# Two of seven half-block products, each made by seven quarter-block products

## The chip, the cores and the metric

The kernel runs on one core of one Trainium2 chip. The metric is the device time of one execution in microseconds. TensorE (PE in the profile) multiplies, with its weight loads shown as PEld; VectorE is DVE, ScalarE ACT, GpSimd POOL, SyncE SP. Everything is float32.

## The reference

Four graph layers run one after the other on x of 128 graphs x 64 nodes x 256 features (8192 tokens in all), each on relu(layernorm(x)) and each added to x. The change touches two places.

Layer 0 ends in LSTMs over windows of length p = 1, 2, 3, 4, with weights of their own for each length, the later ones reading what the earlier have written:

```python
def step(carry, x_t):
    h, c = carry
    g = x_t @ Wih.T + h @ Whh.T + bias          # 256 -> 4 x 256
    i, f, gg, o = jnp.split(g, 4, axis=-1)
    c = jax.nn.sigmoid(f) * c + jax.nn.sigmoid(i) * jnp.tanh(gg)
    h = jax.nn.sigmoid(o) * jnp.tanh(c)
...
for p in range(1, MAX_SKIP + 1):
    wins = h[:, :nw * p, :].reshape(Bv * nw, p, Hd)
    last = _lstm_last(Wih[p-1], Whh[p-1], bih[p-1], bhh[p-1], wins)
    h = h.at[:, jnp.arange(nw) * p + (p - 1), :].set(last.reshape(Bv, nw, Hd))
```

Layer 3 is three times "multiply by a weight, then mix the nodes with adj * adj", with widths 256 -> 512 -> 1024 -> 256 and a relu after the first two:

```python
h = relu(slconv(x, adj, adj, W1)); h = relu(slconv(h, adj, adj, W2)); return slconv(h, adj, adj, W3)
```

Layers 1 (attention) and 2 (a graph convolution with batch norms) lie between them and keep their code.

## The kernel before, in words

**Seven products in place of eight.** A weight block of 2x2 halves, (a11 a12; a21 a22), times an input of 2x2 halves, (b11 b12; b21 b22), needs seven half-block products instead of eight, if sums of the weight halves (`sums`, L228) and differences of the input halves (`differences`, L216) are made first (the Winograd form of Strassen's method). Products 1 to 7 are (a11,b11), (a12,b21), (s4,b22), (a22,t4), (s1,t1), (s2,t2), (s3,t3). `seven` makes them in four PSUM banks: products 1, 5, 6 and 7 first; ACT copies 1 and 5 to SBUF (p1, p5; L181, L182), DVE adds 6 to p1 and 7 to p5 (L184, L185); then `finish` lets POOL add p1 and p5 into the output block 1,1 (L189), adds product 2 into the bank of product 1 for block 0,0, product 3 into that of 5 and product 4 into that of 7, and DVE adds p1 to the last two (L195, L199). `end` is the activation that closes a block.

**LSTM.** Two units (256 windows x 2 blocks each, 224 at length three) are worked in pairs, pair j of each length p. `first_steps` makes step 0, which has no hidden state; `next_step` makes steps t >= 1 of one unit: four input differences (L709 to L714), then two calls of `gate_set`, one for the gates i and g and one for f and o, then cell and hidden state (L721 to L724, `output`). In a gate set of `next_step` the halves of the contraction are x and h, each of two chunks of 128, so one product is four matmuls of 128x128 weights with 128x256 inputs. `blocks_of` makes the weight sums once a length. Lengths one to four have 8, 8, 6 and 4 units.

**Layer 3.** 16 groups of 512 tokens. In each, `second_weights` (512 -> 1024, matmuls at L1599) makes two sets (q = 0 and 2) of seven products, again four matmuls of 128x128 with 128x256 each; the first four products of both sets come before the last three of either. `third_weights` (L1649) follows, with matmuls of 128x128 inputs.

**Order.** The tile framework orders each engine's instructions when the kernel is built: by program order among those that are ready by its own estimate of durations, so that an engine may take a later instruction first. On the chip each engine then keeps that order. There are eight PSUM banks, which is two sets. `tc.issue_after(x)` keeps what follows behind x on its engine. x tiles of the first four groups (tags x0 to x3) are loaded at the start and stay in SBUF until the layer's output is added to them, by DMAs of POOL (L293) in the last pair of length four.

Of the kernel before, what the change touches and what calls it, by code (L numbers as in the profile page):

```python
# [15 lines left out]
P = 128  # L16
# [23 lines left out]
def adj_preln_kernel(ctx: ExitStack, tc: tile.TileContext, x_in, adj, vec, bg0, bg1,  # L40
# [128 lines left out]
    def summed_last():  # L169
        return sums_on_pool[-1]  # L170

    def seven(products, banks, p1, p5, out, end, parts=lambda b: [b]):
# [9 lines left out]
        copied = nc.scalar.copy(p5, ps[1])  # L182

        nc.vector.tensor_tensor(p1, p1, ps[2], ALU.add)  # L184
        added = nc.vector.tensor_tensor(p5, p5, ps[3], ALU.add)  # L185

        def finish():
            sums_on_pool.append(
                nc.gpsimd.tensor_tensor(out=out[1][1], in0=p1, in1=p5, op=ALU.add).ins  # L189
            )  # L190
            end(1, 1, None)
            products[2](ps[0], False)
            end(0, 0, ps[0])
            products[3](ps[1], False)
            nc.vector.tensor_tensor(out[0][1], p1, ps[1], ALU.add)  # L195
            end(0, 1, None)
            products[4](ps[3], False)
            for to, p, q in zip(*(parts(b) for b in (out[1][0], p1, ps[3]))):
                last = nc.vector.tensor_tensor(to, p, q, ALU.add)  # L199
# [116 lines left out]
    with tc.tile_pool(name="lw", bufs=5) as lw:  # L316
# [242 lines left out]
        with tc.tile_pool(name="back", bufs=1, reuse_waits="tile") as back_pool, \  # L559
# [22 lines left out]
            def gate_set(p, n, g, gates, w, bs):  # L582

                pairs = [sevens(w, b, lambda *wb: wb) for b in bs]

                def product(i):
                    def issue(ps, first):
                        for r, j, _ in gates:  # L590
                            for c, (wc, bc) in enumerate(zip(*pairs[r][i])):
                                nc.tensor.matmul(  # L592
                                    ps[:, r], lhsT=wc[:, j, :], rhs=bc,
                                    start=first and r == 0 and c == 0, stop=True,
                                    skip_group_check=True,
                                )

                    return issue

                out = [[g[:, :, m, blk, 0:n] for blk in range(2)] for m in range(2)]  # L600
                p15 = lp.tile([P, 2, 2, 256], F32, tag="p15", name="p15")
                same = gates[0][1:] == gates[1][1:]

                def act(o, ps, j, m, func):
                    col = (p - 1) * 8 + 2 * j + m
                    nc.scalar.activation(o, ps, func, bias=lbias[:, col : col + 1])  # L606
# [10 lines left out]
                return seven(  # L617
                    {i: product(i) for i in range(1, 8)}, [bank((P, 2, 256))[:, :, 0:n] for _ in range(4)],
                    p15[:, 0, :, 0:n], p15[:, 1, :, 0:n], out, end,
                )  # L620

            def output(t, p, u, gate_o, th):
# [78 lines left out]
            def next_step(t, p, n, u, ws, last_sum=None):  # L701

                x_of, cell, hid = u
                tt = dp.tile([P, 4, 2, 256], F32, tag="diff", name="diff")
# [9 lines left out]
                nc.vector.tensor_tensor(ts[3], h1, ts[1], ALU.subtract)  # L714
                if last_sum is not None:
                    last_sum()
                b = (by_chunk([x1]) + [None], by_chunk([h1, h2]), by_chunk(ts))
                ig, fo = gate_tile(), gate_tile()
                gate_i, gate_g, gate_f, gate_o = (g[:, r, :, :, 0:n] for g in (ig, fo) for r in range(2))
                gate_set(p, n, ig, [(0, 0, AF.Sigmoid), (1, 2, AF.Tanh)], ws, [b] * 2)()  # L720
                nc.vector.tensor_tensor(gate_i, gate_i, gate_g, ALU.mult)  # L721
                gate_set(p, n, fo, [(0, 1, AF.Sigmoid), (1, 3, AF.Sigmoid)], ws, [b] * 2)()
# [13 lines left out]
            def blocks_of(p, wi, wh):  # L736
# [14 lines left out]
                return ws, lambda: make([3])  # L751


            stepped = None
            w0 = first_blocks(
                w_next[0], lw.tile([P, 2, 1024], F32, tag="w", name="s"), copied_of[5:9]
            )
            for p, nk in ((1, 8), (2, 8), (3, 7), (4, 8)):
                n = nk * HB
                wi, wh = w_next  # L760
# [5 lines left out]
                for j in range(0, len(units), 2):  # L766
                    two = [unit(p, *u, nk) for u in units[j : j + 2]]
                    first_steps(p, n, two, units[j : j + 2], w0)
                    if p > 1:
                        flush()  # L770
                        if j == 0:
                            ws, last_sum = blocks_of(p, wi, wh)
                    if j + 2 == len(units):
                        if p < 4:
                            w0 = first_blocks(
# [3 lines left out]
                        else:  # L779
# [7 lines left out]
                            nc.vector.tensor_tensor(ss[0], wqk[1][0], wqk[1][1], ALU.add)  # L787
                            nc.vector.tensor_tensor(ss[1], ss[0], wqk[0][0], ALU.subtract)
                            nc.vector.tensor_tensor(wdiff, wqk[0][0], wqk[1][0], ALU.subtract)
                    for t in range(1, p):  # L790
                        for i, u in enumerate(two):
                            stepped_before = stepped
                            stepped = next_step(
                                t, p, n, u, ws, last_sum if (j, t, i) == (0, 1, 0) else None
                            )

                            if p == 4 and j == 2:
# [781 lines left out]
            order=[(2, (2, 3, 0, 1)), (0, range(GT))],  # L1579
        )  # L1580

    def second_weights(m1, room):

        h2 = [arena(ar_right) for _ in range(2)]
# [4 lines left out]
        tt = arena(ar_right).rearrange("p i (c n) -> p i c n", c=2)  # L1589
        ts = [tt[:, i] for i in range(4)]  # L1590
        last = differences(nc.vector, *act[0], *act[1], *ts)

        def products(q):
            def product(w, b):
# [15 lines left out]
        for q in (0, 2):  # L1610
            p1, p5 = (room[:, q + i, :].rearrange("p (r n) -> p r n", r=2) for i in range(2))
            blocks = [
                [h2[m][:, q : q + 2, n * HN : (n + 1) * HN] for n in range(2)] for m in range(2)
            ]
            ends.append(
                seven(
                    products(q), [bank((P, 2, HN)) for _ in range(4)], p1, p5, blocks,
                    ends_in(blocks, AF.Relu),
                )
            )  # L1620
        for end in ends:
# [5 lines left out]
    def third_weights(h2, parts=lambda b: [b]):  # L1627
# [1 line left out]

        last = arena(ar_right)  # L1630
        s3 = last[:, 0:2, :].rearrange("p a (b d) -> p (a b) d", d=D)
        act = [[h2[c][:, :, m * HN : (m + 1) * HN] for c in range(2)] for m in range(2)]
        s_tiles = [arena(ar_right) for _ in range(2)]
        ss = [
            s_tiles[i // 2][:, 2 * (i % 2) : 2 * (i % 2) + 2, :].rearrange(
# [78 lines left out]
                ready += 1  # L1714

    AHEAD = 4
    a, finish_start = first_start()
    s3, scaled = None, None
    for g in range(NG + 1):
# [106 lines left out]
```

## Time and profile before

| | |
|---|---|
| median of three runs | 2432.34 us (2431.85 to 2433.87) |
| the profiled execution | 2432.54 us |
| its span, first to last instruction | 2430.8 us |
| PE, PEld busy | 2409.7 us, 2088.7 us |
| DVE, ACT, POOL busy | 1546.7, 1130.2, 497.5 us |
| L592, matmuls of the LSTM | 156.9 to about 1200 us of the span |
| L1599, matmuls of `second_weights` | 16 groups from 1680.6 us on, about 24.3 us each |
| granted TensorE clock | 0.999 |

A line of the timeline has start, duration (both us), engine, line of the code, operation, tiles out<-in, shape and count of instructions merged into it, and in brackets the idle time of the engine just before it, with what ended it. A group of merged matmuls is shown up to the end of its last one's pipeline, so the next one's start, not start plus duration, tells how fast they follow each other. A matmul of 128*128 weights with 128x256 inputs in float32 shows as two records. `x2` on other engines means two instructions.

### The profile page before, as it was taken

How to read it: one execution, taken by the hardware profiler on the slowest of the kernel's cores; microseconds unless marked ns; L12 is line 12 of the kernel's file. 1: busy time of each engine (PE TensorE's matmuls, PEld its weight loads, DVE VectorE, ACT ScalarE, POOL GpSimd, SP SyncE). 2: the span in 40 equal slices, each digit the busy share in tenths (PEclk: the TensorE clock that was granted, in tenths of full speed). 3: DMA queues.
4: the chain of work that ended last, by engine and by line, in shares of the span. 5: the costliest groups of instructions: out<-in, count | busy, mean ns of one | idle time of the engine just before them, and what ended most of it. 6: DMA issues, size and time to landing. Idle time of an engine off the chain costs nothing.

```text
span 2430.8 us, 46867 instructions
## 1 busy us (share of the span) xinstructions
PE 2409.7 (99%) x19648; PEld 2088.7 (86%) x19648; DVE 1546.7 (64%) x2829; ACT 1130.2 (46%) x2022; POOL 497.5 (20%) x445
## 2 busy tenths in 40 slices
PE   9999999999999999999999999999999999999999
PEld 6778888889999998888888867586988898999898
DVE  6768866666566575575599888576655445444543
ACT  4557755444445343353455565564343333333332
POOL 4432211111111111112224445123111111111100
PEclk9999999999999999999999999999999999999999
DMA  4200000001000000143246410010233100000000
GB/s 140 84 2 1 1 18 1 1 1 35 1 1 1 1 1 1 18 96 70 48 82 129 78 29 2 10 61 10 36 53 62 27 10 19 10 10 11 18 10 19
DMA packets 161587, 73.21 MB, mean 30 GB/s; under 512 B 104416, under 2 KB 157792, under 8 KB 161376
## 3 DMA queue, kind: packets, MB, share of 16 engines
q1 hardware_dynamic: 147984, 57.08, 9.5%
q0 software_dynamic: 12672, 12.58, 3.5%
q8 instruction: 154, 2.52, 0.4%
q10 hardware_dynamic: 720, 0.56, 0.1%
q14 instruction: 57, 0.47, 0.1%
HBM read 40.84 MB, written 20.97 MB: 25 GB/s over the span
## 4 chain that ended last, share of the span: by engine, by line
PE 92%; DVE 5%; ACT 2%; issue 1%; DMA 0%; POOL 0%; ACTq 0%; DVEq 0%; POOLq 0%
PE ps L592 41%; PE ps L1599 16%; PE ps L1649 8%; PE ps L1556 4%; PE ps L146 4%; PE ps L952 3%; PE ps L501 2%; PE ps L527 2%; PE ps L1326 2%; PE ps L878 2%; PE ps L911 2%; PE ps L1388 1%; PE ps L974 1%; PE ps L1670 1%; PE ps L1354 1%
## 5 line engine op out<-in xcount | busy, mean ns | idle before, releaser
L592 PE MATMUL ps<-diff,s 128*128 128x256 f32 (+1 forms) x1824 | 393.5, 371 | 0.9 <-DVE diff L713 0.9
L1599 PE MATMUL ps<-arena 128*128 128x256 f32 x1792 | 391.4, 380 | 0.0
L1599 PEld LDWEIGHTS ps<-arena 128*128 128x128 f32 x1792 | 338.9, 190 | 48.2 <-issue 2.0
L592 PEld LDWEIGHTS ps<-diff,s 128*128 128x128 f32 x1824 | 345.9, 190 | 33.8 <-issue 1.6
L606 ACT ACTIVATE gates<-gates,lbias 128x512 f32<-128x512 f32 (+5 forms) x426 | 244.1, 620 | 200.5 <-DVE gates L195 144.8
L189 POOL TENSOR_TENSOR gates<-p 128x512 f32<-128x512 f32 (+1 forms) x115 | 148.6, 1292 | 882.0 <-DVE p L185 831.1
L592 PE MATMUL ps<-h,w 128*128 128x256 f32 (+1 forms) x1028 | 241.0, 371 | 0.0
L592 PE MATMUL ps<-diff,w 128*128 128x256 f32 (+1 forms) x1040 | 238.7, 370 | 0.0
L189 POOL TENSOR_TENSOR arena<-arena 128x512 f32<-128x512 f32 (+1 forms) x80 | 91.1, 1139 | 613.7 <-DVE arena L185 601.4
L592 PEld LDWEIGHTS ps<-diff,w 128*128 128x128 f32 x1040 | 197.4, 190 | 18.2
L592 PEld LDWEIGHTS ps<-h,w 128*128 128x128 f32 x1028 | 195.0, 190 | 19.2 <-issue 0.5
L606 ACT ACTIVATE gates<-ps,lbias 128x256 f32<-128x256 f32 (+3 forms) x213 | 91.8, 477 | 247.2 <-PE ps L592 247.0
L239 ACT ACTIVATE arena<-arena 128x512 f32<-128x512 f32 x144 | 88.5, 628 | 250.4 <-POOL arena L189 163.1
L195 DVE TENSOR_TENSOR gates<-p,ps 128x512 f32<-128x512 f32 (+1 forms) x115 | 76.3, 664 | 114.3 <-PE ps L592 114.0
L1649 PE MATMUL ps<-arena 128*128 128x128 f32 x1280 | 148.4, 275 | 0.0
L1649 PEld LDWEIGHTS ps<-arena 128*128 128x128 f32 x1280 | 146.5, 192 | 0.9
L184 DVE TENSOR_TENSOR arena<-arena,ps 128x512 f32<-128x512 f32 (+1 forms) x80 | 48.2, 602 | 138.5 <-PE ps L1599 50.0
L195 DVE TENSOR_TENSOR arena<-arena,ps 128x512 f32<-128x512 f32 (+1 forms) x80 | 48.1, 602 | 125.5 <-PE ps L1599 57.6
L228 DVE TENSOR_TENSOR arena<-arena 128x512 f32<-128x512 f32 (+1 forms) x192 | 108.2, 597 | 21.9 <-ACT arena L239 20.2
L592 PE MATMUL ps<-state,w 128*128 128x256 f32 (+1 forms) x512 | 116.1, 370 | 0.9 <-ACT p L181 0.8
L184 DVE TENSOR_TENSOR p<-p,ps 128x512 f32<-128x512 f32 (+1 forms) x131 | 86.9, 663 | 47.4 <-PE ps L592 46.6
L199 DVE TENSOR_TENSOR gates<-p,ps 128x512 f32<-128x512 f32 (+1 forms) x115 | 76.6, 666 | 62.9 <-PE ps L592 62.4
(219 smaller groups left out, 4127.1 us busy)
## 6 DMA issues: line engine op xcount, KB each, us to landing
x<-in_x SPq DMA_DIRECT2D x19, 512.0 KB, 4.1
y<-turned SPq DMA_DIRECT2D x64, 128.0 KB, 3.7
v<-vt SPq DMA_DIRECT2D x128, 64.0 KB, 2.3
w<-in_wih SPq DMA_DIRECT2D x4, 1024.0 KB, 8.4
x_for_h<-in_x SPq DMA_DIRECT2D x8, 512.0 KB, 6.6
x<-y POOLq DMA_DIRECT2D x8, 512.0 KB, 6.3
x_for_h<-y POOLq DMA_DIRECT2D x8, 512.0 KB, 6.8
z<-w SPq DMA_DIRECT2D x64, 64.0 KB, 2.0
```

The lines of the kernel that those rows point to most:

```text
L146: last = nc.tensor.matmul(pss[b][half * 64 : half * 64 + 64, c, t, :], lhsT=src[rows, t, col : col + 64], rhs=a2[rows, :], start=True, sto ...
L184: nc.vector.tensor_tensor(p1, p1, ps[2], ALU.add)
L189: nc.gpsimd.tensor_tensor(out=out[1][1], in0=p1, in1=p5, op=ALU.add).ins
L195: nc.vector.tensor_tensor(out[0][1], p1, ps[1], ALU.add)
L199: last = nc.vector.tensor_tensor(to, p, q, ALU.add)
L228: last = eng.tensor_tensor(out=s, in0=p, in1=q, op=op)
L239: nc.scalar.activation(o, o, func)
L592: nc.tensor.matmul(ps[:, r], lhsT=wc[:, j, :], rhs=bc, start=first and r == 0 and c == 0, stop=True, skip_group_check=True,)
L606: nc.scalar.activation(o, ps, func, bias=lbias[:, col : col + 1])
L1556: nc.tensor.matmul(ps[:, t, :], lhsT=w[:, t * P : (t + 1) * P], rhs=b, start=first and t == 0, stop=True, skip_group_check=True,)
L1599: nc.tensor.matmul(ps[:, r, :], lhsT=w[:, c, col : col + P], rhs=b[:, c, :], start=first and r == 0 and c == 0, stop=c == 1, skip_group_ch ...
L1649: nc.tensor.matmul(ps[:, t, :], lhsT=w[:, c, t * P : (t + 1) * P], rhs=b[:, c, :], start=first and t == 0 and c == 0, stop=c == 3, skip_gr ...
```

## The change

Products 6 and 2 of `seven` are each made by seven quarter-block products themselves: of 128x128 weights with 128x128 inputs, seven where eight would do the same. This is done in `next_step` for length two, for length four in the first of its two pairs, and in `second_weights` from group 4 on. In one bank the four quarters get m1, m5, m7 and m6; ACT and DVE read these out (`common`), POOL adds the shared sum to three quarters of the result; m2, m3, m4 are then added to the first three quarters in the bank (`last`), and DVE adds those 384 columns to the result (`rest`). For product 2, p1 is copied a second time, into the output block, and the activation of that block now reads SBUF. The quarter differences are made in place of part of t2 and h1, by DVE, in each step (`split_differences`, four each); the quarter sums of the weights once for each length and once in layer 3. They live in the x tiles: in the LSTM in x0 to x3, which are loaded a second time after the first pair of length four; in layer 3 in x0 to x2, whose groups are written out by then. Two layouts change so that four quarters lie side by side: the gates' tile (from r, m, k, n to m, k, r, n) and h2.

```diff
+    class Split:
+        def __init__(self, w, b, u):
+            (a11, a12), (_, a22), ss = w
+            (b11, _), (b21, b22), ts = b
+            self.m = (
+                None, (a11, b11), (a12, b21), (ss[3], b22), (a22, ts[3]),
+                (ss[0], ts[0]), (ss[1], ts[1]), (ss[2], ts[2]),
+            )
...
+        def products(self, ps, which, first=False):
+            _, q = self.quarters(ps)
+            for k, i in enumerate(which):
+                w, b = self.m[i]
+                nc.tensor.matmul(
+                    q[k], lhsT=w, rhs=b, start=first and k == 0, stop=True, skip_group_check=True
+                )
+        def first(self, ps):
+            self.products(ps, (1, 5, 7, 6), True)
+        def common(self, ps, to):
+            _, q = self.quarters(ps)
+            flat, t = self.quarters(to)
+            nc.scalar.copy(self.u, q[0])
+            nc.vector.tensor_tensor(self.u, self.u, q[3], ALU.add)
+            for k in (1, 2):
+                nc.vector.tensor_tensor(t[3], t[3], q[k], ALU.add)
+            three = flat[:, self.h :].rearrange("p (i n) -> p i n", n=self.h)
+            nc.gpsimd.tensor_tensor(
+                out=three, in0=three, in1=self.u.unsqueeze(1).to_broadcast([P, 3, self.h]),
+                op=ALU.add,
+            )
+        def last(self, ps):
+            self.products(ps, (2, 3, 4))
+        def rest(self, ps, to):
+            flat, pf = (self.quarters(t)[0][:, 0 : 3 * self.h] for t in (to, ps))
+            return nc.vector.tensor_tensor(flat, flat, pf, ALU.add)
+
+    def split_differences(eng, t, ts):
+        h = t.shape[-1] // 2
+        (b11, b12), (b21, b22) = ([t[:, c, k * h : (k + 1) * h] for k in range(2)] for c in range(2))
+        t1, t2, t4 = (ts[:, i, 0:h] for i in range(3))
+        for o, p, q in ((t1, b12, b11), (t2, b22, t1), (b12, b22, b12), (t4, b21, t2)):
+            eng.tensor_tensor(out=o, in0=p, in1=q, op=ALU.subtract)
...
     def seven(...):
         for i, p in zip((1, 5, 6, 7), ps):
-            products[i](p, True)
+            if split and i == 6:
+                split[6].first(p)
+            else:
+                products[i](p, True)
         nc.scalar.copy(p1, ps[0])
         copied = nc.scalar.copy(p5, ps[1])
-        nc.vector.tensor_tensor(p1, p1, ps[2], ALU.add)
+        if split:
+            nc.scalar.copy(out[0][0], ps[0])
+            split[6].common(ps[2], p1)
+        else:
+            nc.vector.tensor_tensor(p1, p1, ps[2], ALU.add)
         added = nc.vector.tensor_tensor(p5, p5, ps[3], ALU.add)
         def finish():
+            if split:
+                split[6].last(ps[2])
+                split[6].rest(ps[2], p1)
             sums_on_pool.append(nc.gpsimd.tensor_tensor(out=out[1][1], in0=p1, in1=p5, op=ALU.add).ins)
             end(1, 1, None)
-            products[2](ps[0], False)
-            end(0, 0, ps[0])
+            if split:
+                split[2].first(ps[0])
+                split[2].common(ps[0], out[0][0])
+            else:
+                products[2](ps[0], False)
+                end(0, 0, ps[0])
             products[3](ps[1], False)
             nc.vector.tensor_tensor(out[0][1], p1, ps[1], ALU.add)
             end(0, 1, None)
+            if split:
+                split[2].last(ps[0])
+                split[2].rest(ps[0], out[0][0])
+                end(0, 0, None)
             products[4](ps[3], False)
...
-                return lp.tile([P, 2, 2, 2, 256], F32, tag="gates", name="gates", bufs=3)
+                gates = lp.tile([P, 2, 2, 2, 256], F32, tag="gates", name="gates", bufs=3)
+                return gates.rearrange("p m k r n -> p r m k n")
...
                 # next_step, behind the four differences
+                if within:
...
+                    tb = {
+                        6: split_differences(nc.vector, ts[1], room[:, 0:3]),
+                        2: split_differences(nc.vector, h1, room[:, 3:6]),
+                    }
...
                 # blocks_of
                 make(range(3))
+                if p != 3:
+                    within = {}
+                    for i, a, s in ((6, ss[1], free[0]), (2, wm[:, 0], free[1])):
+                        blocks = [[a[:, c, 2 * r : 2 * r + 2] for c in range(2)] for r in range(2)]
+                        s = s.rearrange("p a (i f) -> p a i f", f=P)
+                        split_sums(nc.vector, blocks, s)
+                        within[i] = blocks, s
...
+                    if p == 4 and j == 2:
+                        within = None
+                        for g in range(NK):
+                            xs[g] = xpool.tile([P, GT, D], F32, tag=f"x{g}", name=f"x{g}")
+                            load_x(xs[g], g)
...
+    SPLIT_FROM = 4
-            h2, behind = second_weights(m1, h1)
+            h2, behind = second_weights(m1, h1, within)
+            if g == SPLIT_FROM - 1:
+                with tc.issue_after(behind):
+                    within = split_second()
```

More of the change, by code (lines that the diff above doesn't have):

```diff
@@ L170, in summed_last, with quarters @@
         return sums_on_pool[-1]
-    def seven(products, banks, p1, p5, out, end, parts=lambda b: [b]):
+    class Split:
[6 more added lines that the diff above has]
+            )
+            self.u, self.h = u, u.shape[-1]
+        def quarters(self, t):
+            flat = t.rearrange("p r n -> p (r n)")
+            return flat, [flat[:, i * self.h : (i + 1) * self.h] for i in range(4)]
+        def products(self, ps, which, first=False):
[24 more added lines that the diff above has]
+            return nc.vector.tensor_tensor(flat, flat, pf, ALU.add)
@@ L178, in seven, with split_weights @@
+    def split_weights(blocks, s, k):
+        (a11, a12), (_, a22) = ([b[:, k] for b in row] for row in blocks)
+        return (a11, a12), (None, a22), [s[:, i, k] for i in range(4)]
+    def seven(products, banks, p1, p5, out, end, parts=lambda b: [b], split=None):
         ps = banks
         for i, p in zip((1, 5, 6, 7), ps):
-            products[i](p, True)
+            if split and i == 6:
+                split[6].first(p)
+            else:
+                products[i](p, True)
         nc.scalar.copy(p1, ps[0])
@@ L618, in gate_set @@
                     {i: product(i) for i in range(1, 8)}, [bank((P, 2, 256))[:, :, 0:n] for _ in range(4)],
-                    p15[:, 0, :, 0:n], p15[:, 1, :, 0:n], out, end,
+                    p15[:, 0, :, 0:n], p15[:, 1, :, 0:n], out, end, split=split,
                 )
@@ L757, in adj_preln_kernel @@
             )
+            free = [xpool.tile([P, GT, D], F32, tag=f"x{g}", name=f"free{g}") for g in range(NK)]
             for p, nk in ((1, 8), (2, 8), (3, 7), (4, 8)):
```

66 lines of the change are left out of this document (54 added, 12 removed).

## The prediction, made before the change was built

> **What bounds the kernel now.** I read the page first, its busy table, its chain that ended last and its costliest groups.
>
> ```profile
> span 2430.8 us, 46867 instructions
> PE 2409.7 (99%) x19648; PEld 2088.7 (86%) x19648; DVE 1546.7 (64%) x2829; ACT 1130.2 (46%) x2022; POOL 497.5 (20%) x445
> ...
> PE 92%; DVE 5%; ACT 2%; issue 1%; DMA 0%; POOL 0%; ACTq 0%; DVEq 0%; POOLq 0%
> ```
>
> PE is busy but for 21 us, and the chain is PE's own. PE time saved is time saved, as long as nothing makes PE wait. So I need two things: what a small matmul costs beside a large one, and what PE would wait for. The timeline of PE over one group of layer 3 has both sizes, back to back:
>
> ```profile
> 2012.59 24.44 PE L1599 MATMUL ps<-arena 128*128 128x256 f32 x112
> 2036.86 5.52 PE L1649 MATMUL ps<-arena 128*128 128x128 f32 x48
> 2042.22 1.95 PE L1649 MATMUL ps<-w,arena 128*128 128x128 f32 x16
> 2044.01 3.74 PE L1649 MATMUL ps<-arena 128*128 128x128 f32 x32
> 2047.58 1.95 PE L1649 MATMUL ps<-w,arena 128*128 128x128 f32 x16
> 2049.37 0.38 PE L1556 MATMUL ps<-arena 128*128 128x256 f32 x1
> ```
>
> Go by the starts, since matmuls overlap. The 112 small ones take 2049.37 - 2036.86 = 12.51 us, 0.1117 us each. The 112 large ones include an entry wait; in the LSTM 56 of them take 12.085 us (904.77 to 916.85 in the timeline), 0.2158 each. One f32 matmul of the code is two records: seven half-block products of four matmuls are 56 records.
>
> Next, the timeline of DVE and ACT in one LSTM gate set, whose p5, p6 and p7 start on PE at 490.99:
>
> ```profile
> 490.25 1.33 ACT L606 ACTIVATE gates<-gates,lbias 128x512 f32<-128x512 f32 x2 [0.88 <-DVE gates L199]
> 491.67 1.22 DVE L721 TENSOR_TENSOR gates<-gates 128x1024 f32<-128x1024 f32 x1 [1.52 <-ACT gates L606]
> 492.92 0.59 ACT L182 COPY p<-ps 128x512 f32<-128x512 f32 x1 [0.87 <-PE ps L592]
> 494.72 0.69 DVE L184 TENSOR_TENSOR p<-p,ps 128x512 f32<-128x512 f32 x1 [1.82 <-PE ps L592]
> 496.44 0.69 DVE L185 TENSOR_TENSOR p<-p,ps 128x512 f32<-128x512 f32 x1 [1.04 <-PE ps L592]
> ```
>
> DVE waits for PE here, not PE for DVE. Last, the one place of length two where the planner's order left PE waiting, and a DVE subtraction beside a POOL addition:
>
> ```profile
> 521.21 1.89 PE L592 MATMUL ps<-diff,s 128*128 128x256 f32 x8
> 523.20 1.99 PE L592 MATMUL ps<-state,w 128*128 128x256 f32 x8
> 525.03 1.89 PE L592 MATMUL ps<-state,s 128*128 128x256 f32 x8
> 527.28 3.69 PE L592 MATMUL ps<-diff,s 128*128 128x256 f32 x16 [0.36 <-DVE diff L713]
> ...
> 947.87 1.59 POOL L189 TENSOR_TENSOR gates<-p 128x512 f32<-128x512 f32 x1 [11.38 <-DVE p L185]
> 948.37 1.64 DVE L714 TENSOR_TENSOR diff<-state,diff 128x512 f32<-128x512 f32 x1
> ```
>
> PE made p2 and p3 (state) ahead of p6 and p7 (diff,s x16): the planner does fill waits with other products. Even so PE lost 0.26 + 0.10 + 0.36 = 0.72 us there (gaps between one group's expected end, start + 8 x 0.2158, and the next start).
>
> **Matmuls removed and added.** A split product has 14 small records for 8 large: 8 x 0.2158 - 14 x 0.1117 = 1.726 - 1.564 = 0.163 us saved. How many: length two has 8 units of one step, length four 2 units (pair j = 0) of 3 steps, so 14 steps of 2 gate sets with 2 split products each, 56; layer 3 has 12 groups (4 to 15) of 2 sets, 48. Gain 9.1 + 7.8 = **16.9 us**.
>
> **The new waits, per split product.** PE can't add m2, m3 and m4 into the bank before ACT and DVE have read m1, m5, m7 and m6 out of it. The chain: PE to reader 0.28 (p6 ended 490.99 + 16 x 0.2158 = 494.44, L184 began 494.72); ACT copy of 128x128, 0.27 (128x512 0.57 and 128x256 0.37, halved on); ACT to DVE 0.09 (491.58 to 491.67); three DVE additions of 128x128, 0.285 each (0.69 at 512, 0.42 at 256) and 0.2 apart, 0.69; DVE to PE 0.15 (L713 ended 527.13, PE began 527.28). Sum 1.48 us. The cover is one product of eight records, p7 for product 6 and p3 for product 2: 1.73. Slack **0.25 us**, if DVE and ACT are free. Behind the late matmul PE holds its whole queue, in the order built in.
>
> Are they free? The windows answer gives DVE 27.78 of 48.35 us in four sets of length two, and 82.45 of 143.0 in the twelve of length four: 57%, 7.0 us a set. Added per set: three additions for one at product 6 (+0.17), three at product 2 (0.86), two wide ones of 128x384 (0.56 each), and half of eight subtractions a step (8 x 0.26 / 2 = 1.04): 3.2 us. DVE stands at 10.2 of 11.76 us, 87% by durations, which overlap by 0.09 an instruction, so nearer 75%. It isn't evenly spread: the set after a step's end carries cell, hidden state and differences, some 8 us that now meet the new additions; the other set is free. So of a step's two sets I charge one. Its price is bounded by 0 (the planner fills in) and the 0.72 of the reordered place; I take the middle row, the 0.36 wait: 14 x 0.36 = **5.0 us** (0 to 10.1). It can't fall below nothing: the whole L592 line stands idle 5.8 us now.
>
> In layer 3 the second set's p1, p5, p6, p7 follow the first set's on PE, so only product 2's wait counts, 24 times; DVE is at 48% (22.23 of 46.00). Near the slack, I take 0.1: **2.4 us** (0 to 24 x 0.36 = 8.6).
>
> **POOL.** Each split product adds a 128x384 addition, about 1.0 us (between 0.73 at 256 and 1.27 at 512), 104 in all. DVE's wide addition waits for it, in order, and p4's or the output's additions stand behind. In the free set it ends some 0.3 us before the matmuls it must meet, so I charge nothing; uncovered, it is 0.3 a product, inside the bounds above. But the last two lines show what POOL does to a DVE subtraction beside it: 1.64 for 0.69. The Trainium skill's page "SBUF — State Buffer" (section "SBUF: two separate sides") says why: the two engines share a port pair, and a DVE operation with two SBUF inputs waits out the whole of a POOL operation that holds it. That speaks against this change: by the rule, 104 holds of up to 0.95 us would take up to 99 us of DVE's time, and should a quarter reach PE, the gain would be gone; by the row, a hold in the full set (L714, L713) has cost PE nothing so far.
>
> **Weight sums, once a layer.** Eight DVE additions of 128x256 (0.42, 0.33 apart), 2.7 us, ahead of the first step's differences. At length two DVE is busy 17.16 of 18.80 us there (302.8 to 321.6), so 1.1 us slips onto PE; length four and layer 3 have room, 0.4 for both: **1.5 us** (0 to 8.1, all three bare).
>
> **At nothing.** The gates' and h2's new layout changes strides, not element counts. ACT copies p1 twice (+0.57 a set) at 46% load, into a gap of 0.87. Product 2's activation reads SBUF instead of PSUM (0.50 for 0.47). The reload of four x tiles (512 KB, 4.1 us each to landing) goes on SP after pair 0 of length four, some 48 us before POOL's DMAs add into them; without that cover POOL's queue would hold the set sums behind it, up to 4 x 4.1 = 16 us once.
>
> **Sum:** -16.9 + 5.0 + 2.4 + 1.5 = -8.0. The profiled execution took 2432.54 (span 2430.8 and 1.7 around it), the median is 2432.34: about 2424.5.
>
> **Rivals.** *Waits win, slower.* In place of PE's own pace the chain ACT, DVE, PE sets the step: if one 128x512 DVE operation (0.60 apart) stands ahead of the additions each time, all 56 + 24 waits are 0.35 late, 28 us, net +11: 2443.5. It decides from 16.9 / 80 = 0.21 us a wait, a chain of 1.94 for 1.73 of cover. For it: 87%, the holds, thin slack. Against: the other four banks, and the order at 523 us. *Half of that,* 14 us: 2429.5, no change to be measured. *All covered,* only the weight sums paid: 2417. That splitting happens less often than counted is told by the records, and the diff leaves no doubt of it.
>
> **How the numbers follow.** Forecast 0.45 (own range 2420 to 2428), all covered 0.17, half 0.17, slower 0.21. A measurement of this kernel tells about 0.2%, 4.9 us, from no change: faster 0.62, same 0.17, slower 0.21. The range runs from all covered, 2417, to 2440, short of the slower rival's end.
>
> **What would show it.** 1456 records of 128x128 at the new line and 832 fewer of 128x256; PE busy near 2393; DVE near 1720 (52 sets x 2.16, 26 steps x 2.1, sums 10); four LSTM sets in 47.0 us plus waits instead of 48.35; waits of PE on DVE in the split lines of about 0.36 in one set of a step and none in the other. If the four take over 48.35, the waits won. I am wrong on size if small matmuls mixed with large don't keep 0.1117.

## The result: slower, and the profile after

The changed kernel took 2441.6 us (median of five runs, 2440.11 to 2445.75), the kernel before beside it 2431.85: 1.0044 times as long [1.0029, 1.0058], 9.8 us more by the medians. (Here and below, differences in us are of medians; the ratio and its 95% interval are of the means.) That is outside the range of the prediction (2417 to 2440) and on the other side of no change from its forecast, 2424.5. The profiled execution is the shortest of the five, 2440.11.

The page of the changed kernel, the lines that answer to the first three shown of before:

```profile
span 2438.3 us, 49036 instructions
PE 2404.0 (99%) x20272; PEld 2090.9 (86%) x20272; DVE 1703.7 (70%) x3425; ACT 1181.3 (48%) x2178; POOL 609.1 (25%) x549
...
PE 82%; DVE 13%; ACT 3%; issue 1%; POOL 1%; SPq 0%; DMA 0%; DVEq 0%; ACTq 0%; POOLq 0%
```

DVE's share of the chain that ended last went from 5 to 13%. PE is called 99% busy in both kernels, so the busy share tells nothing here; the chain and the waits do. The answer on the waits of PE (engine, line and releaser; us in total, times, longest) begins with two lines that the kernel before cannot have, since their matmuls are new:

```profile
PE ps L191 <- DVE arena L204: 5.0, 12, 0.7
PE ps L191 <- DVE p L204: 4.3, 5, 1.1
```

L191 makes the quarter products, L204 is the last small addition of DVE in `common`. "arena" is layer 3, "p" is product 6 in the LSTM. These totals count from the modelled end of a matmul. From start to start, less the usual distance, the twelve waits of layer 3 are 6.97 us, and all waits on L204 in the LSTM 9.2 us.

Where nothing waits, the set is as fast as foretold. One gate set of length two in the timeline of PE:

```profile
357.08 1.89 PE L672 MATMUL ps<-h,w 128*128 128x256 f32 x8
...
368.84 1.03 PE L672 MATMUL ps<-h,w 128*128 128x256 f32 x4
```

From the first product of this set to that of the next: 368.84 - 357.08 = 11.76 us, a quarter of the 47.0 foretold for four sets. So the gain is there and is given back. By starts of PE's matmuls the span divides as follows (us; "expected" is before less the gross gain of 0.163 us for each split product: 32 at length two, 24 at length four, 48 in layer 3):

| stage | before | expected without waits | after |
|---|---|---|---|
| lengths 1 and 2 | 411.91 | 406.7 | 416.75 |
| length 3 (unchanged) | 304.03 | 304.03 | 304.01 |
| length 4 | 327.00 | 323.1 | 328.59 |
| layers 1 and 2 (unchanged) | 480.73 | 480.73 | 479.10 |
| layer 3, from the first matmul of `second_weights` | 746.43 | 738.6 | 748.79 |

The new waits are thus 10.1 us at length two, 5.5 at length four and 10.2 in layer 3, 25.8 together, against 8.9 in the prediction.

**A wait of layer 3, close up.** The timeline of PE, DVE and POOL in one group of layer 3 (L307 makes the input sums for `third_weights`, 128x512, of two SBUF operands; L260 is POOL's addition of p1 and p5 into block 1,1):

```profile
2037.32 2.32 PE L1738 MATMUL ps<-arena 128*128 128x256 f32 x10
2040.01 0.46 PE L191 MATMUL ps<-arena 128*128 128x128 f32 x2 [0.36 <-DVE arena L204]
...
2038.08 0.28 DVE L204 TENSOR_TENSOR arena<-arena,ps 128x128 f32<-128x128 f32 x1
2038.28 1.38 DVE L307 TENSOR_TENSOR arena<-arena 128x512 f32<-128x512 f32 x1
2039.58 0.27 DVE L204 TENSOR_TENSOR arena<-arena,ps 128x128 f32<-128x128 f32 x1
...
2037.51 1.61 POOL L260 TENSOR_TENSOR arena<-arena 128x512 f32<-128x512 f32 x1 [3.49 <-DVE arena L216]
```

Between the two additions that PE waits for, DVE's order has an L307. It takes 1.38 us instead of 0.68 (its row when POOL is silent is shown under the second experiment) and ends 0.54 after POOL's L260 (2037.51 + 1.61 = 2039.12; 2038.28 + 1.38 = 2039.66). All twelve waits look like this, each with an L307 held by 0.70 to 0.72. The additions themselves, with one operand in PSUM, keep their 0.28 beside the same POOL operation. The hold of 0.70 less the slack of 0.25 makes 0.45; measured are 0.52 to 0.54 in ten groups and 0.81 and 0.83 in two. After each of the twelve, the second record follows the first by 0.18 us instead of 0.11, 0.07 more that isn't in these figures.

**A wait of the LSTM, close up.** The timeline of POOL, DVE, ACT and PE at length four (L206: POOL's shared addition in `common`; L202 and L204: DVE's small additions there; L216: `rest`; L201: ACT's copy of m1; L816: a product of gates; L224: a quarter difference):

```profile
904.72 1.00 POOL L206 TENSOR_TENSOR p<-p,free 128x384 f32<-128x384 f32 x1 [11.20 <-DVE p L204]
906.81 1.27 POOL L260 TENSOR_TENSOR gates<-p 128x512 f32<-128x512 f32 x1 [1.09 <-DVE p L216]
908.04 1.45 POOL L206 TENSOR_TENSOR gates<-gates,free 128x384 f32<-128x384 f32 x1
909.52 0.55 DVE L216 TENSOR_TENSOR gates<-gates,ps 128x384 f32<-128x384 f32 x1 [0.89 <-POOL gates L206]
910.11 2.13 ACT L686 ACTIVATE gates<-gates,lbias 128x256 f32<-128x256 f32 x4 [1.64 <-DVE gates L216]
912.28 1.22 DVE L816 TENSOR_TENSOR gates<-gates 128x1024 f32<-128x1024 f32 x1
913.57 0.27 ACT L201 COPY free<-ps 128x128 f32<-128x128 f32 x1
914.43 0.28 DVE L224 TENSOR_TENSOR free<-state,free 128x128 f32<-128x128 f32 x1
914.63 0.28 DVE L202 TENSOR_TENSOR free<-free,ps 128x128 f32<-128x128 f32 x1
...
915.58 0.46 PE L191 MATMUL ps<-diff,s 128*128 128x128 f32 x2 [1.08 <-DVE p L204]
```

Between POOL's late addition and PE's wait no DVE operation is held; POOL's queue is what is late. Product 2's shared addition stands behind the block sum on POOL, is itself drawn out to 1.45, and ends at 909.49. DVE's L216, in order, waits 0.89 for it, and ACT's activations wait 1.64 for L216. L816 begins as they end, six quarter differences follow it on DVE, the last at 914.43, and only then come the additions: L202 begins at 914.63, though the copy that it reads had ended at 913.84. From L216 on DVE hardly stands still, so its 0.89 are passed on to PE, some 6 us later; the other 0.36 of the 1.25 from start to start are DVE's own work ahead of the additions.

Of the 19 waits on L204 in the LSTM three are of this kind, 1.25 each. Eight others, 0.27 to 0.33, have a held difference of inputs (L789, L790) ahead of the additions. In two more, 0.27 and 0.42, it is an operation that makes the hidden state (L713). In the remaining six, 0.25 to 0.83, none of the DVE operations just ahead of the additions is held: ACT's copy or DVE's own work comes late. The experiments tell how much of all this is owed to POOL.

### The profile page after: what moved, and what is told of

Its sections match the earlier page's. It is cut to its first block, busy times and chain, and to the rows that moved or that the text cites. A ratio compares the mean times of both kernels' runs of the same rounds, so it can differ in the third digit from the quotient of the medians.

```text
span 2438.3 us, 49036 instructions
## 1 busy us (share of the span) xinstructions
PE 2404.0 (99%) x20272; PEld 2090.9 (86%) x20272; DVE 1703.7 (70%) x3425; ACT 1181.3 (48%) x2178; POOL 609.1 (25%) x549
## 4 chain that ended last, share of the span: by engine, by line
PE 82%; DVE 13%; ACT 3%; issue 1%; POOL 1%; SPq 0%; DMA 0%; DVEq 0%; ACTq 0%; POOLq 0%
PE ps L672 34%; PE ps L1738 9%; PE ps L1788 8%; PE ps L191 5%; PE ps L1666 4%; PE ps L146 3%; PE ps L580 2%; PE ps L1062 2%; PE ps L606 2%; PE ps L1436 2%; PE ps L988 2%; PE ps L1021 2%; DVE arena L307 2%; PE ps L1498 1%; PE ps L1084 1%
## 5 line engine op out<-in xcount | busy, mean ns | idle before, releaser
L686 ACT ACTIVATE gates<-gates,lbias 128x512 f32<-128x512 f32 (+3 forms) x482 | 267.2, 606 | 229.2 <-DVE gates L270 175.1
L672 PE MATMUL ps<-diff,s 128*128 128x256 f32 (+1 forms) x1600 | 349.8, 370 | 0.5 <-DVE diff L793 0.5
L672 PEld LDWEIGHTS ps<-diff,s 128*128 128x128 f32 x1600 | 301.1, 190 | 26.1 <-issue 0.9
L1738 PE MATMUL ps<-arena 128*128 128x256 f32 x1408 | 320.5, 380 | 0.0
L260 POOL TENSOR_TENSOR gates<-p 128x512 f32<-128x512 f32 (+1 forms) x115 | 146.5, 1274 | 605.5 <-DVE p L253 527.3
L1738 PEld LDWEIGHTS ps<-arena 128*128 128x128 f32 x1408 | 260.5, 190 | 34.2 <-issue 1.7
L260 POOL TENSOR_TENSOR arena<-arena 128x512 f32<-128x512 f32 (+1 forms) x80 | 95.5, 1193 | 481.7 <-DVE arena L253 401.7
L318 ACT ACTIVATE arena<-arena 128x512 f32<-128x512 f32 x168 | 103.9, 629 | 145.7 <-POOL arena L260 67.7
L1788 PEld LDWEIGHTS ps<-arena 128*128 128x128 f32 x1280 | 146.6, 192 | 1.1 <-ACT arena L318 0.2
L686 ACT ACTIVATE gates<-ps,lbias 128x256 f32<-128x256 f32 (+2 forms) x157 | 68.1, 478 | 145.4 <-PE ps L672 145.2
L307 DVE TENSOR_TENSOR arena<-arena 128x512 f32<-128x512 f32 (+1 forms) x192 | 120.2, 639 | 8.1 <-ACT arena L318 4.0
L672 PE MATMUL ps<-state,s 128*128 128x256 f32 (+1 forms) x512 | 116.8, 369 | 0.0
L270 DVE TENSOR_TENSOR arena<-arena,ps 128x512 f32<-128x512 f32 (+1 forms) x80 | 47.9, 598 | 92.6 <-PE ps L1788 49.3
L246 ACT COPY arena<-ps 128x512 f32<-128x512 f32 (+1 forms) x80 | 41.1, 514 | 132.7 <-PE ps L1738 57.4
```

Source lines behind the costliest of these rows:

```text
L307: last = eng.tensor_tensor(out=s, in0=p, in1=q, op=op)
L318: nc.scalar.activation(o, o, func)
L672: nc.tensor.matmul(ps[:, r], lhsT=wc[:, j, :], rhs=bc, start=first and r == 0 and c == 0, stop=True, skip_group_check=True,)
L1738: nc.tensor.matmul(ps[:, r, :], lhsT=w[:, c, col : col + P], rhs=b[:, c, :], start=first and r == 0 and c == 0, stop=c == 1, skip_group_ch ...
L1788: nc.tensor.matmul(ps[:, t, :], lhsT=w[:, c, t * P : (t + 1) * P], rhs=b[:, c, :], start=first and t == 0 and c == 0, stop=c == 3, skip_gr ...
```

## Experiments

Each difference is against the kernel before, run beside it on the same chip. Three theories of the 25.8 us were put against each other. **HOLDS** (called POOL in later expectations): the waits come from POOL, whose additions hold DVE's operations or are late themselves. **BACKLOG** (called LOAD later): DVE has too much to do; POOL's work put on DVE would then make it worse. **COVER:** the order leaves too little work of PE between the small products and their partners in the same bank.

### Where: one part of the change at a time

The splits in the LSTM alone:

```diff
-    SPLIT_FROM = 4
+    SPLIT_FROM = 100
```

> The split is kept in the LSTM and left out in layer 3. Two theories stand for the time the change costs. HOLDS: the matmuls that add m2, m3 and m4 wait, because between the DVE additions that free their bank the planner has put an SBUF-only DVE operation, and a POOL addition holds that one up for about 0.7 us. BACKLOG: DVE simply has too many operations ahead of those additions, POOL or not. Both see the stages as separate: by the starts in the trace of the change, the LSTM stages there take 6.5 us more than before (4.9 at lengths one and two, 1.6 at length four). So 2431.9 + 6.5 = 2438.4, 2436 to 2442; the layer 3 groups back to 24.28 us of second-weight matmuls each. If the two places hurt each other, it is under 2435.

The splits in layer 3 alone:

```diff
-                if p != 3:
+                if p > 4:
```

> The split is kept in layer 3 and left out in the LSTM, weight sums included; the x tiles are still loaded twice. Both theories: layer 3 takes 2.4 us more than before in the trace of the change, so 2434.3, 2432 to 2437. Each of the 12 groups should again show one wait of 0.53 to 0.83 us of PE on the last addition of product 2, with one weight sum on DVE held for about 0.7 us in front of it. If the second load of x costs anything on the critical path, it shows as time above 2434 outside layer 3.

LSTM alone: 2439.88 against 2431.77, +8.1 us, 1.0032 [1.0020, 1.0045]. Layer 3 alone: 2435.70, +3.9 us, 1.0015 [1.0006, 1.0024]. The stages repeat the table above within 2 us: lengths 1 and 2 at 416.75 in the first (411.91, as before, in the second), layer 3 at 750.77 in the second (746.61 in the first). The two losses add up to 12.0, about the 9.8 of the whole: the parts don't harm each other, and each alone pays more than it gains.

### Which engine: POOL's additions on DVE

The addition of p1 and p5, in the split products' sets:

```diff
-                nc.gpsimd.tensor_tensor(out=out[1][1], in0=p1, in1=p5, op=ALU.add).ins
+                (nc.vector if split else nc.gpsimd).tensor_tensor(
+                    out=out[1][1], in0=p1, in1=p5, op=ALU.add
+                ).ins
```

> In split sets alone, the sum of p1 and p5 goes from POOL (1.27 us) to DVE (about 0.68 us). HOLDS: this POOL addition is the one that holds the weight sum in each group of layer 3, so the wait of 0.53 there should shrink to under 0.15 in most of the 12 groups: 5 to 7 us less than the change's 2441.6, about 2435.5; the LSTM's waits of 0.27 to 0.33, where the other POOL addition is the holder, stay. BACKLOG: DVE gets 52 x 0.6 = 31 us more, ahead of or among the additions: layer 3's waits stay or grow, 2442 to 2450.

2433.31 against 2431.77: +1.5 us, 1.0008 [0.9999, 1.0016], some 8 us better than the change as it was, where HOLDS had 5 to 7. The timeline of the same place in layer 3 (L309 is the L307 of above; the file has two lines more):

```profile
2035.49 0.28 DVE L204 TENSOR_TENSOR arena<-arena,ps 128x128 f32<-128x128 f32 x1
2035.68 0.68 DVE L309 TENSOR_TENSOR arena<-arena 128x512 f32<-128x512 f32 x1
2036.29 0.28 DVE L204 TENSOR_TENSOR arena<-arena,ps 128x128 f32<-128x128 f32 x1
...
2034.12 2.75 PE L1740 MATMUL ps<-arena 128*128 128x256 f32 x12
2036.72 0.46 PE L191 MATMUL ps<-arena 128*128 128x128 f32 x2
```

DVE's order there is the same but for the sum of p1 and p5, which is now DVE's own and stands further ahead. The same L307 stands between the two additions, but it takes 0.68 and PE doesn't wait. All twelve waits of layer 3 on L204 are gone. So in layer 3 it was not the operation ahead of the additions that cost, as the prediction's slower rival has it, but its hold.

The shared addition of `common`:

```diff
-            nc.gpsimd.tensor_tensor(
+            nc.vector.tensor_tensor(
                 out=three, in0=three, in1=self.u.unsqueeze(1).to_broadcast([P, 3, self.h]),
```

> The addition of the shared sum to three quarters (104 of them, 1.0 us each on POOL) goes to DVE (about 0.55 us each). HOLDS: the seven LSTM waits of 0.27 to 0.33 behind a held subtraction go, about 2.6 us with their restarts; the twelve waits of layer 3 (0.53, the holder there is the sum of p1 and p5) stay: about 2439, 2436 to 2441. BACKLOG: DVE gets 104 x 0.5 = 52 us more: PE waits grow everywhere, 2446 to 2460. If both act, layer 3 stays and the LSTM gains at the held places and loses at the full ones: about 2443.

2432.17 against 2431.77: +0.4 us, 0.9999 [0.9990, 1.0007], about 9 us better than the change as it was. BACKLOG is wrong in sign: DVE got more work and PE waited less. HOLDS expected about 7 us less of a gain, since it priced the holds and not POOL's queue: without the shared additions in it, DVE's `rest` finds no late POOL, and the waits on L204 in the LSTM fall from 9.2 us to 2.5, the one shown above from 1.25 to 0.30. Not all of that need be POOL: with each edit the framework orders DVE anew, and at this place only two of the six quarter differences still stand ahead of the additions. In layer 3, where POOL keeps L260, they stay (5.96 us from start to start, for 6.97). A group of layer 3 in this kernel:

```profile
2029.45 1.39 DVE L307 TENSOR_TENSOR arena<-arena 128x512 f32<-128x512 f32 x1
...
2028.67 1.61 POOL L260 TENSOR_TENSOR arena<-arena 128x512 f32<-128x512 f32 x1 [4.50 <-DVE arena L216]
2031.18 0.46 PE L191 MATMUL ps<-arena 128*128 128x128 f32 x2 [0.31 <-DVE arena L204]
```

Both on DVE (the two edits together):

> In split sets, both POOL additions (the sum of p1 and p5, and the shared sum into three quarters) go to DVE; POOL has nothing to do there. POOL theory (POOL additions hold DVE's two-SBUF-input operations, and DVE's wide addition waits in order for POOL's queue of three): the two single moves gained 8.3 and 9.4 us in different waits, so together about 17: 2424, 2421 to 2427, with the last additions' waits nearly gone in both places. LOAD theory (what matters next is DVE's own work, now 83 us more than in the change): the second move gives back what it takes, 2430 to 2436.

2424.59 against 2432.61: -8.0 us, 0.9964 [0.9950, 0.9978]. The two edits bring 8.3 and 9.4 us alone and 17.8 together, as POOL theory had it. From the page:

```profile
PE 2398.6 (99%) x20272; PEld 2093.6 (86%) x20272; DVE 1756.5 (72%) x3581; ACT 1183.0 (49%) x2178; POOL 429.4 (18%) x393
```

DVE has 53 us more to do than in the changed kernel (1756.5 against 1703.7), POOL 180 less, and no wait on L204 is left in the answer on waits. The stages are 409.59, 323.76 and 739.66: 2.9, 0.7 and 1.1 us above those expected without waits. That is 21.1 us less than in the changed kernel; the whole gained less because this profiled execution spent 6 us more in layers 1 and 2, where the edits do nothing, 2.2 us of it in one wait there for which the profile shows no cause. What is left in layer 3 is of another kind: seven split groups have a wait of 0.22 us for a quarter difference (L224), and the last one has 0.62. With slower second records these make the twelve groups 3.2 us longer than 12 x 23.63; the stage shows 1.1, since stretches without splits were 2.1 shorter than before.

The same choice of engine in sets whose products are not split (the sums of p1 and p5 on DVE, and nothing else of the change but layouts and copies of x):

> A control. The products, matmul for matmul, are those of the kernel before; the new layouts of the gates and of h2 and the second load of x stay, and in the sets that the change would split the sum of p1 and p5 is on DVE. If the mend is a mend of the split (POOL theory), it does nothing here, where PE never waited for those additions: 2431 to 2434, and the LSTM and layer 3 stages as before within 0.5 us. If moving the sum to DVE were a gain of its own, or the layouts a cost of their own, it would be under 2429, or over 2435.

2432.69 against 2433.34: -0.7 us, 1.0000 [0.9991, 1.0009]. Without the splits it makes no measurable difference which engine adds p1 and p5. The prediction's observation, that a hold had cost PE nothing so far, fits the kernel before; it was no price for a kernel in which PE waits for DVE in the middle of a set.

### How much cover: another order

Products 7 and 6 change places, product 6's last three quarters go behind product 2's first four and product 3, and product 2's last three behind product 3 and product 6's last:

```diff
-        for i, p in zip((1, 5, 6, 7), ps):
+        for i, p in zip((1, 5, 7, 6), (ps[0], ps[1], ps[3], ps[2])) if split else zip((1, 5, 6, 7), ps):
...
             if split:
+                split[2].first(ps[0])
+                split[2].common(ps[0], out[0][0])
+                products[3](ps[1], False)
                 split[6].last(ps[2])
                 split[6].rest(ps[2], p1)
...
```

The cover is then 8 x 0.1117 + 8 x 0.2158 = 2.62 us for product 6 and 8 x 0.2158 + 6 x 0.1117 = 2.40 for product 2, against 1.73 (four quarter products are 8 small records, three are 6; a whole product is 8 large ones).

> POOL keeps its additions. Only the order of the program, and so the planner's priorities, differs in split sets: products 1, 5, 7, then the first four of 6; the first four of 2, product 3, the last three of 6, the last three of 2, product 4. The additions of product 6 now have 2.6 us of other matmuls as cover in the set (first four of 2, product 3), those of product 2 have 2.4 (product 3, last three of 6), for 1.73 before. COVER theory (a thin cover turned every delay on DVE into a wait, whoever caused it): the waits before the last additions go, some 12 us in the LSTM and 8 in layer 3: about 2422. POOL theory: DVE still waits in order for POOL's queue, each set ends later, and ACT's copies for the next set come late: 2428 to 2436.

2429.26 against 2432.61: -3.3 us, 0.9987 [0.9978, 0.9996]. Half of each theory: the LSTM's stages come to 408.79 and 323.64, as COVER has it, and no wait on L204 is left there, with POOL as loaded as before. Layer 3 is worse than in the changed kernel, 749.81: each of its twelve split groups has a wait on L204 of 0.95 or 0.96 from start to start. One of them (POOL's sum of p1 and p5 is L263 in this file):

```profile
2021.68 1.30 POOL L263 TENSOR_TENSOR arena<-arena 128x512 f32<-128x512 f32 x1 [0.74 <-DVE arena L216]
2024.19 0.69 DVE L307 TENSOR_TENSOR arena<-arena 128x512 f32<-128x512 f32 x1 [1.47 <-ACT arena L318]
...
2026.40 0.69 DVE L307 TENSOR_TENSOR arena<-arena 128x512 f32<-128x512 f32 x1
2027.00 0.28 DVE L204 TENSOR_TENSOR arena<-arena,ps 128x128 f32<-128x128 f32 x1
2027.42 0.46 PE L191 MATMUL ps<-arena 128*128 128x128 f32 x2 [0.80 <-DVE arena L204]
```

The L307 between the additions takes 0.69, so these waits are not holds. What is late is again POOL, by a third path: DVE stands 1.47 us before the first L307 for ACT's activations (L318), and these begin 0.03 us after POOL's sum has ended (2021.68 + 1.30 = 2022.98; L318 at 2023.01). DVE then has three L307 and one addition of 128x512 to do ahead of the last small addition. Whether it is POOL or that load, the next run tells.

The new order with the sum of p1 and p5 on DVE, and then with both:

> The order of late_order with only the sum of p1 and p5 on DVE; the shared sum's addition stays on POOL. If one POOL addition a product under the longer cover is harmless (POOL theory with the queue of three as the main part), it is about 2415, as fast as with both moved, 2413 to 2417. If the shared addition still holds or delays the last additions under that cover, 2418 to 2424. If the order alone made the waits of 0.95 in layer 3, they stay here and it is 2424 or more.

> The order of late_order and both additions on DVE. If cover and POOL are the two halves of the same waits, one mend is enough and this one is as fast as the better of the two, within 2 us: about 2421. If they are different waits, 2417 to 2420, near the full gain of 16.9 less the weight sums and first steps. If DVE's load is next, 2425 or more.

With the sum on DVE: 2419.41 against 2433.34, -13.9 us, 0.9946 [0.9933, 0.9958], and the twelve waits of layer 3 are gone. (The time falls in the range whose reading was that the shared addition still delays the last ones; the trace has one such wait, 0.76 us in the LSTM.) The same four operations of 128x512 still stand ahead of the last small addition, but DVE no longer stands before them, and that addition begins 20.94 us after the group's first matmul instead of 21.76 (21.17 in one group). So it was POOL's late sum that PE waited for, and not the load on DVE. With both: 2413.80 against 2432.61, **-18.8 us, 0.9924 [0.9911, 0.9936]**, the fastest kernel here and below all that was expected of it. Its page:

```profile
span 2414.2 us, 48973 instructions
PE 2395.3 (99%) x20272; PEld 2096.4 (87%) x20272; DVE 1757.3 (73%) x3581; ACT 1177.1 (49%) x2178; POOL 429.9 (18%) x393
...
PE 94%; DVE 4%; ACT 1%; issue 0%; POOL 0%; DVEq 0%; ACTq 0%; POOLq 0%
```

The chain is PE's again, 94% against 82%. The matmuls of `second_weights` take 23.62 us a split group, where 24.28 - 4 x 0.163 = 23.63 is the full gain, and the LSTM's stages 408.07 and 323.38 come within 1.7 us of it. In this profiled execution, the slowest of the five (2416.02), the three split stages are 16.9 us shorter than before (layer 3 comes to 736.9), about 1.7 of it in layer 3's stretches without splits. That the medians differ by 18.8, more than the gross gain, is no finding: the interval reaches from 15.6 to 21.7 us. Between the two kernels with the new order POOL's shared addition still costs 4.9 us by the medians, and in the two traces hardly at the split matmuls: 1.7 in the LSTM's two stages, 3.4 in layer 3 outside `second_weights`, where most of the stretches that follow take 22.67 us in place of 22.50.

### The gross gain

The quarter products alone: `common`, `rest` and the quarter differences' subtractions are left out, so that PE has nothing new to wait for.

> Leaves out, in split products, ACT's copy of the shared quarter, DVE's additions, POOL's addition and the quarter differences (the small matmuls take the quarters themselves as inputs); all matmuls of the change and the weight sums stay. It prices the gross term. If mixed small matmuls keep 0.112 us and large ones 0.216: before less 16.9 plus at most 1.5 for the weight sums: 2415 to 2417, with no waits in the split matmuls but for the first steps' differences. If mixing them costs more, or the split sets need their banks in ways that have nothing to do with the additions, 2422 or more.

2420.88 against 2432.61: -11.7 us, 0.9953 [0.9940, 0.9966], some 4 to 6 less than expected. The split stages are where the working put them: 407.13 at lengths 1 and 2 (406.7), 323.08 at length four (323.1), 23.62 a group in `second_weights` (23.63). What is missing lies in code without splits: the stretches of layer 3 between `second_weights` of one group and the next sum to 253.4 us from group 4 on, against 250.8 before and 250.2 in the fastest kernel; the unsplit groups and their stretches take 0.4 us more together than before, layers 1 and 2 also 0.4, and the LSTM begins 0.6 later. Such a stretch takes between 21.5 and 24.1 us, in other groups in other kernels; what decides it stays open. It is why totals of single kernels here aren't read to better than some 3 us, and stages are.

## Why the prediction was wrong, step by step

- **PE's gain, 16.9 us: right.** The waiting line has its 1456 records of 128x128, DVE is busy 1703.7 us (about 1720 foretold), a set without a wait takes 11.76 us, and with the additions left out all three stages fall by what was worked out. Small matmuls keep 0.1117 among large ones.
- **POOL, "I charge nothing": the step that failed.** It should have been about 18 us by the medians (from +9.8 to -8.0 us as both additions leave POOL), 21 by the changed stages. With 18 in its place the sum -8.0 becomes +10, and measured are +9.8; that it fits so closely is partly luck, since other terms were off (below). Both ways in which POOL costs were in the text and were set aside: the hold, because "a hold" had cost PE nothing so far (the trace of before has 35 held operations of 128x512 or 128x448, but none in layer 3, where the changed kernel waits for one in each split group), and the queue, because in the free set POOL "ends some 0.3 us before". The unsplit run shows why the first was no evidence: without the split products, where PE doesn't need DVE in the middle of a product, the choice of engine for the sum of p1 and p5 changes nothing that could be measured. The prediction had the slack of 0.25 and a hold of 0.95 two paragraphs apart; held against each other they give 0.7 us a product where they meet, and the slower side. Of the second, the prediction costed the POOL addition of one product, not the three POOL operations of a set one behind the other (1.00, then 1.27 and 1.45 back to back above) with DVE's in-order wait at the end.
- **The rule that spoke against the change was right.** The Trainium skill, page "SBUF — State Buffer", section "SBUF: two separate sides", has a DVE operation with two SBUF inputs wait out the POOL operation that holds the shared ports. The rows agree but for a little: 1.38 for 0.68, ended 0.54 us after POOL's end, where a wait for all of it and its own 0.68 after it would make 0.68. Not a quarter of 99 us reached PE, but 18 to 21 us did, holds and late additions of POOL together.
- **The full set, 5.0 us, and layer 3, 2.4: too small as measured (15.6 with the sums of weights, and 10.2), near without POOL, but by other waits.** With both additions on DVE the stages are 2.9 + 0.7 + 1.1 = 4.7 us above those without waits (6.8 with the 3.2 us of layer 3's split groups for its 1.1), against 5.0 + 2.4 + 1.5 charged. The waits that were charged, for the last additions, are gone there: so the slack of 0.25 held. What is left at length two stands mostly in the reordered place (1.28 us for an input difference, 0.74 for ACT's second copy of p1, which the prediction put at nothing), and in layer 3 at the quarter differences. That the totals are near is luck.
- **The 0.36 was misread.** By the prediction's own rule the third gap is 527.28 - (525.03 + 8 x 0.2158) = 0.52, and the place loses 0.88; 0.36 counts from the modelled end. The charge would have been 14 x 0.52 = 7.3 us and the sum -5.7: still faster, so this isn't the step that failed.
- **The weight sums, 1.5 us: rather too much.** One wait can be put down to them, 0.48 us at 324 us, at length two's start: PE stands for an activation (L686) that itself stood 1.38 for DVE, whose order has the sums of weights in front. It is there with the additions left out too (0.49), and not with the splits in layer 3 alone. At length four's start and in layer 3's first split group none stands out.
- **The slower rival, 2443.5, came near in time, by another mechanism.** It had a 128x512 operation of DVE ahead of the additions each time. Such operations do stand there, and in layer 3 they cost nothing at 0.68 us (sum on DVE); they cost when POOL doubles them. It also had 80 waits of 0.35; there are 31 on L204 (19 in the LSTM, 12 in layer 3), 0.52 on the mean (16.2 / 31).
- **PE busy near 2393: wrong (2404.0).** With both additions on DVE the same 20272 matmuls show 2398.6, in the fastest kernel 2395.3, and without the additions 2392.3. So the busy time rises with the waits, and a saving in matmuls can't be read from it alone.

## What to carry to other kernels

When a change puts an operation of another engine between two uses of one PSUM bank, put the slack of that chain beside every disturbance the trace shows of its engines, a held operation or a queue, even where they cost nothing today: cover that hid them is what such a change spends. Work given to an idle engine isn't free: here POOL stood at 25%, and moving 180 us off it to a DVE at 70% gained 18 us. And when the busy share doesn't move, look at the chain that ended last and at single sets without a wait, which tell the gain from what is given back.

## What the runs showed of the hardware

- A DVE operation with both inputs in SBUF that meets a POOL addition ends at a fixed distance after POOL's end, whenever it began: 0.54 to 0.56 us for 39 of the 50 held operations of 128x512 in the changed kernel (the other eleven met a second POOL instruction and end as far after the first), 0.48 to 0.49 for all ten of 128x448, their own times (0.68 and 0.61) less 0.13. The row shown of before has it too (948.37 + 1.64 is 0.55 after 947.87 + 1.59). One with an input in PSUM keeps its time beside the same POOL operation (0.28); of the 702 of 128x512 in the changed kernel none takes over 0.69. POOL's addition is drawn out too: 1.56 to 1.72 us instead of 1.27 for 128x512, in the 20 cases where such a DVE operation with two SBUF inputs was under way as it began.
- After a wait of PE the second record starts 0.18 us after the first instead of 0.11, in each of layer 3's twelve.
- Single additions of 128x384 took 0.55 on DVE and 1.00 on POOL.
